# A gated expert layer and FFN: the FFN's first layer as seven products of quarters, over blocks of 1024 tokens

## The chip, the cores and the metric

The kernel runs on one core of a Trainium2 chip. A core has a matrix engine (TensorE, PE in the profile, with its weight loads shown apart as PEld), a vector engine (VectorE, DVE), an engine for activation functions and copies (ScalarE, ACT), a general engine (GpSimd, POOL) and a queue engine that issues DMAs (SyncE, SP). They run their own instruction streams in order and wait for one another by semaphores. Matrix products are written to PSUM[...]; everything else lies in SBUF. The metric is the device time of one execution in microseconds (us); before the change it is 289.29 us, the median of three runs (288.32 to 289.66).

## The reference

Input x is 4 x 512 tokens of 512 numbers. Two layers follow, each with a residual and a gate:

```python
x = x + tanh(g_xattn) * xattn(layernorm(x), ids, ctx, ctx, ctx)
x = x + tanh(g_ffn) * ffn(layernorm(x), w1, w3, w2, wr)
```

In xattn every token has one of four experts by its id (three bounds: 6250, 12500, 18750). Expert e is the 512 x 512 matrix ctx[e], used three times: g = silu(h ctx[e]^T), u = h ctx[e]^T, y = (g * u) ctx[e]^T. In ffn, h = silu(silu(h w1^T) w3^T) w2^T for all 2048 tokens, with 512 x 512 matrices, and a router (softmax of h wr^T, the best two of eight) gives two gates a token. `out.at[indices].add(gates * h)` adds those rows to rows 0 to 7 of the output, so that all tokens end in eight rows: the second layer's outputs can be summed by gate first and multiplied by w2 once.

## The kernel before

The tokens are sorted by expert into 17 passes of 128 rows. Thirteen passes (0 to 12) belong wholly to one expert each and need one matrix; four (13 to 16) hold the rests in groups of 32 rows and need four matrices, one for each group. The tables for this (`padded`, `lanes`, `atlane`, `what`, `tok`, lines 178 to 330) are computed on DVE at the start; `tok`, a product in PSUM, is the list of rows, from which `from_row` (gather) and `to_row` (scatter) are made. Meanwhile `busy(n)` gives PE filler products.

A pass p goes through: `gather` (POOL, an indirect DMA, line 393), `centre` (DVE: statistics and subtraction), `turn_in` (four PE transposes into a PSUM tile "tp", an ACT copy to hT), `up` (product z with the matrix, line 457; silu on ACT; a DVE multiply gives g), `turn_mid` (transposes of g, copy to gT), `down` (product y with the same matrix; DVE adds it to x, line 485; POOL scatters the row to the output), `norms` (DVE: the second layer norm), and `turn_out` (transposes, and ACT copies into hT2, the FFN's input; for a pass of 32-row groups four small copies to computed columns, line 533).

`load(p)` puts the matrices of a pass, 1 MB each, on SP's queue into the buffers of pool `mp` (8). A matrix is used by `up` and by `down`, and its buffer is free when `down` has read it; SP waits for that in its own order.

The order of the work is written out by hand and each engine runs in the order of the program. `order` is 0 to 6, 13, 7, 8, 14, 9, 10, 15, 11, 12, 16; "index" below is a place in this list, and the loop (lines 747 to 768) does for i: up(i), turn_in(i+1), centre(i+2), gather and load(i+3), down(i-1), turn_out(i-2), norms, a step of the FFN, turn_mid(i), another step. A step is the next piece of `ffn(b)`, a generator for a block of 512 tokens which enters the list `running` once all its passes are turned out (before: at i = 5, 10, 16 and 18). Its pieces are: four of the first layer (product u with w1, four matmul calls over 512 tokens, line 591, then silu into s1), one with the router's logits lg (line 604) and the routing on DVE, four of the second layer (product v with w3, line 618, silu into s2), and a short one in which the gated sums are added to `acc`. What has not run by the end of the loop runs after it. PSUM's eight banks are four for products ("mm": cnt, idle, tok, z, y, u, v, o in the order in which they are made), three for transposes and one for acc.

Of the kernel before, what the change touches and what calls it, by code (L numbers as in the profile page):

```python
# [8 lines left out]
F32 = mybir.dt.float32  # L9
BF16 = mybir.dt.bfloat16  # L10
F16 = mybir.dt.float16
I32 = mybir.dt.int32
AF = mybir.ActivationFunctionType
ALU = mybir.AluOpType
# [4 lines left out]
P = 128  # L19
# [5 lines left out]
def tile_gated_moe_ffn(  # L25
# [50 lines left out]
    assert E == 4 and G == 4  # L76
    TB = 512
    NB = NT // TB
    TT = TB // P

    const = ctx.enter_context(tc.tile_pool(name="const", bufs=1))
    mp = ctx.enter_context(tc.tile_pool(name="mp", bufs=8))
    hp = ctx.enter_context(tc.tile_pool(name="hp", bufs=2))
    xp = ctx.enter_context(tc.tile_pool(name="xp", bufs=5))
    work = ctx.enter_context(tc.tile_pool(name="work", bufs=3))
    s1p = ctx.enter_context(tc.tile_pool(name="s1p", bufs=2))
    small = ctx.enter_context(tc.tile_pool(name="small", bufs=4))
    ps_mm = ctx.enter_context(tc.tile_pool(name="ps_mm", bufs=4, space=bass.MemoryType.PSUM))
    ps_tp = ctx.enter_context(tc.tile_pool(name="ps_tp", bufs=3, space=bass.MemoryType.PSUM))
    ps_acc = ctx.enter_context(tc.tile_pool(name="ps_acc", bufs=1, space=bass.MemoryType.PSUM))  # L90

    def ct_(shape, dtype, name):
        return const.tile(list(shape), dtype, tag=name, name=name)

# [32 lines left out]
    for e in range(1, E):  # L127
# [12 lines left out]
    H = 12  # L140
    lane = ct_([P, P, H], BF16, "lane")
    nc.gpsimd.iota(
        lane, pattern=[[1, P], [0, H]], base=0, channel_multiplier=0,
        allow_small_or_imprecise_dtypes=True,
    )
    passes = ct_([P, NP, NJ], F16, "passes")
    nc.gpsimd.iota(
        passes, pattern=[[P, NP], [0, NJ]], base=0, channel_multiplier=0,
        allow_small_or_imprecise_dtypes=True,
    )  # L150

# [38 lines left out]

    idle = ps_mm.tile([P, TB], F32, tag="mm", name="idle")

    def busy(n):
        for _ in range(n):
            nc.tensor.matmul(
                idle, ones, lane.rearrange("p a b -> p (a b)")[:, 0:TB], start=True, stop=True
            )

# [29 lines left out]

    terms = ct_([P, 3, E, NJ], F32, "terms")
    over = ct_([P, E, NJ], F32, "over")  # L230
    nc.vector.tensor_tensor(over, rank_in, wide(size[:, 0, :]), ALU.is_ge)
    jump = ct_([P, E], F32, "jump")
    nc.vector.tensor_sub(jump, cut[:, E : 2 * E], cut[:, 1 : E + 1])
    nc.vector.tensor_mul(terms[:, 0], rank_in, hot)
    nc.vector.tensor_mul(over, over, hot)
    nc.vector.tensor_tensor(terms[:, 1], hot, wide(cut[:, 0:E]), ALU.mult)
    nc.vector.tensor_tensor(terms[:, 2], over, wide(jump), ALU.mult)
    padded = ct_([P, NJ], I32, "padded")
    with nc.allow_low_precision("whole numbers below 4096"):
        nc.vector.tensor_reduce(padded, terms.rearrange("p h e j -> p j (h e)"), AX.X, ALU.add)  # L240
    inpass_i = ct_([P, NJ], I32, "inpass_i")
    nc.vector.tensor_single_scalar(inpass_i, padded, -P, op=ALU.bitwise_and)

    start = ct_([P, 2 * E - 1], F32, "start")
    nc.vector.scalar_tensor_tensor(start, cut[:, 1 : 2 * E], 0.0, steps, ALU.is_le, ALU.mult)
    lanes = ct_([P, NJ], BF16, "lanes")
    nc.vector.tensor_sub(lanes, padded, inpass_i)
    which0 = ct_([P, 1], I32, "which0")
    with nc.allow_low_precision("whole numbers below 4096"):
        nc.vector.tensor_reduce(which0, start, AX.X, ALU.add)  # L250
    atlane = [ct_([P, P, n], F16, f"atlane{n}") for n in (H, NJ - H)]

# [9 lines left out]
    at_lane(0)  # L262
    inpass = ct_([P, NJ], F16, "inpass")
    nc.vector.tensor_copy(inpass, inpass_i)
    what = ct_([P, NP, NJ], F16, "what")
# [35 lines left out]

    busy(25)
    from_row = ct_([P, NP], I32, "from_row")
# [6 lines left out]
    def row_tables():  # L310
# [19 lines left out]
        )  # L330


    hT2 = {NB - 1: ct_([P, KC, TB + Q], F32, "hT2")}
    acc = ps_acc.tile([P, D], F32, tag="acc", name="acc")
# [76 lines left out]
    def turn_in(p):  # L411
        tp = transposed(hs.pop(p), f"a{p}")
        hTs[p] = work.tile([P, KC * P], F32, tag="hT", name=f"hT_{p}")
        nc.scalar.copy(hTs[p], tp)

    def first_in(p):

        st = small.tile([P, 6], F32, tag="st", name=f"st_a{p}")
        nc.vector.bn_stats(st, xs[p])
        mvs[p] = small.tile([P, 2], F32, tag="mv", name=f"mv_a{p}")  # L420
        nc.vector.bn_aggr(mvs[p], st)
        hTs[p] = work.tile([P, KC * P], F32, tag="hT", name=f"hT_{p}")
        n = D // 2
        for i in range(2):
            h = work.tile([P, n], F32, tag="h", bufs=4, name=f"h_a{p}_{i}")
            nc.vector.tensor_scalar(
                h, xs[p][:, i * n : (i + 1) * n], mvs[p][:, 0:1], None, ALU.subtract
            )
            tp = ps_tp.tile([P, n], F32, tag="tp", name=f"tp_a{p}_{i}")
            for k in range(n // P):  # L430
                nc.tensor.transpose(tp[:, k * P : (k + 1) * P], h[:, k * P : (k + 1) * P], ident)
            nc.scalar.copy(hTs[p][:, i * n : (i + 1) * n], tp)  # L432
# [32 lines left out]
    def up(p, inside=None):  # L465
        z = ps_mm.tile([P, D], F32, tag="mm", name=f"z_{p}")
        expert_product(z, hTs.pop(p), p, inside)
        g = work.tile([P, D], F32, tag="g", name=f"g_{p}")
        rs = rss.pop(p)
        nc.scalar.activation(g, z, AF.Silu, scale=rs)  # L470
        nc.vector.scalar_tensor_tensor(g, z, rs, g, ALU.mult, ALU.mult)  # L471
        gs[p] = g

    def turn_mid(p):
        tp = transposed(gs.pop(p), f"g{p}")
        gT = work.tile([P, KC * P], F32, tag="gT", name=f"gT_{p}")
        nc.scalar.copy(gT, tp)
        gTs[p] = gT
# [35 lines left out]
    def turn_out(p):  # L514

        tp = transposed(hs2.pop(p), f"f{p}").rearrange("p (k t) -> p k t", k=KC)
        if p < NF:
            b = p // TT
            if b not in hT2:
                hT2[b] = hp.tile([P, KC, TB], F32, tag="hT2", name=f"hT2_{b}")  # L520
            nc.scalar.copy(hT2[b][:, :, p % TT * P : (p % TT + 1) * P], tp)  # L521
            return
# [11 lines left out]

    def route(b, lg):


# [23 lines left out]

        lt = small.tile([P, TT, Q], F32, tag="lt", bufs=2, name=f"lt_{b}")
        nc.vector.transpose(lt.rearrange("p t q -> p (t q)"), lg)  # L563
        l1 = lt[:, :, 0:NR]
# [18 lines left out]

    def ffn(b):

        hT = hT2.pop(b)
        s1 = s1p.tile([P, KC, TB], F32, tag="s1", name=f"s1_{b}")
        for m in range(KC):
            u = ps_mm.tile([P, TB], F32, tag="mm", name=f"u_{b}_{m}")
            for k in range(KC):  # L590
                nc.tensor.matmul(  # L591
                    u,
                    w1[:, k, m * P : (m + 1) * P],
                    hT[:, k, 0:TB],
                    start=(k == 0),
                    stop=(k == KC - 1),
                )
            nc.scalar.activation(s1[:, m, :], u, AF.Silu)  # L598
            yield
        lg = ps_tp.tile([P, P], F32, tag="tp", name=f"lg_{b}")  # L600
        for k in range(KC):
            cols = hT[:, k, 0:TB].rearrange("p (t c) -> p t c", t=TT)
            for i in range(P // Q):
                nc.tensor.matmul(  # L604
                    lg[i * Q : (i + 1) * Q, :],
                    wr[:, k, :],
                    cols[:, :, i * Q : (i + 1) * Q],
                    start=(k == 0),
                    stop=(k == KC - 1),
                )  # L610
        g = route(b, lg)
        yield
        def gated(t, half=None):

            c0, n = (0, D) if half is None else (half * D // 2, D // 2)
            v = ps_mm.tile([P, n], F32, tag="mm", name=f"v_{b}_{t}_{c0}")
            for k in range(KC):
                nc.tensor.matmul(  # L618
                    v,
                    s1[:, k, t * P : (t + 1) * P],  # L620
                    w3[:, k, c0 : c0 + n],
                    start=(k == 0),
                    stop=(k == KC - 1),
                )
            s2 = work.tile([P, n], F32, tag="s2", bufs=5, name=f"s2_{b}_{t}_{c0}")
            nc.scalar.activation(s2, v, AF.Silu)  # L626
            return s2

        def add(t, s2):
# [4 lines left out]
                start=(b == 0),  # L634
                stop=(b == NB - 1 if t < TT - 2 else b == NB - 2),
            )
# [12 lines left out]
        s2s = []  # L649
        if b < NB - 1:  # L650
            for t in range(TT):
# [9 lines left out]
        for t in range(TT - 2):  # L661
            add(t, s2s[t])
        a = work.tile([P, D], F32, tag="a", bufs=1, name="a")
        nc.scalar.copy(a, acc)
# [39 lines left out]
    SHORT = 1  # L704
    last = {b: max(i for i, p in enumerate(order) if min(p // TT, NB - 1) == b) for b in range(NB)}
    running = []

# [39 lines left out]
    for i in range(2, NP + 2):  # L747
# [16 lines left out]
        step()  # L764
        running += [ffn(b) for b in range(NB) if last[b] == i - 2]
        if i < NP:
# [55 lines left out]
```

## Time and profile before

| | |
|---|---|
| median of three runs | 289.29 us |
| profiled execution | 289.3 us, its span (first to last instruction) 287.6 us |
| granted TensorE clock, mean | 0.997 |
| PE busy | 278.1 us (97%) |
| DVE busy | 128.9 us (45%) |
| ACT busy | 63.9 us (22%) |
| POOL busy | 38.8 us (14%) |
| first layer, u (L591), PE | 57.1 us |
| second layer, v (L618), PE | 57.3 us |
| expert products z and y (L457), PE | 61.8 and 61.4 us |
| DMA | 42.54 MB, mean 148 GB/s over the span |

A line of instructions in the profile names the source line, the engine, the operation, output and inputs, partitions x elements, and a count; then the busy time, the mean of one in ns, and the idle time just before, with what ended it. "A<-B" means that A is made from B. The mean of one matmul is longer than the step from one to the next, because matmuls overlap; steps are read from the times at which they start.

### The profile page before, as it was taken

The numbers are of one execution on the slowest core, as the hardware profiler recorded it, in microseconds if no ns is written. First come the engines' busy times: TensorE is split into PE (matmuls) and PEld (weight loads), VectorE is DVE, ScalarE is ACT, GpSimd is POOL, SyncE is SP. The second block draws the span as 40 slices with busy tenths as digits, with TensorE's granted clock in tenths as the row PEclk, the third lists the DMA queues.
The fourth block names the chain that finished last, engine by engine and source line by source line (L and its number), as shares of the span: only waits on it lengthen the run. The fifth ranks groups of instructions, "written<-read, shape, count | busy, mean of one in ns | idle before, by whom it ended". The sixth has DMA issues, their size and how long they took to land.

```text
span 287.6 us, 3554 instructions
## 1 busy us (share of the span) xinstructions
PE 278.1 (97%) x1192; PEld 129.1 (45%) x1193; DVE 128.9 (45%) x573; ACT 63.9 (22%) x122; POOL 38.8 (14%) x62
## 2 busy tenths in 40 slices
PE   4999999999999999999999999999999999999994
PEld 1444455554434544434444445444443454344463
DVE  4379878773707660807270866170533431001300
ACT  2015221332111322213212232212321221111120
POOL 6420122221111111111111111010110100000000
PEclk9999999999999999999999999999999999999998
DMA  0575999996512349622359634044000000000000
GB/s 1 190 285 186 384 391 390 391 391 252 201 55 113 106 177 397 232 78 93 126 160 385 232 98 182 0 157 171 36 0 36 13 0 1 0 0 2 0 1 2
DMA packets 20722, 42.54 MB, mean 148 GB/s; under 512 B 2143, under 2 KB 2207, under 8 KB 20704
## 3 DMA queue, kind: packets, MB, share of 16 engines
q1 hardware_dynamic: 17664, 33.66, 32.4%
q0 software_dynamic: 2720, 8.65, 8.3%
q8 instruction: 9, 0.15, 0.2%
q14 instruction: 9, 0.07, 0.1%
q10 hardware_dynamic: 320, 0.01, 0.1%
HBM read 38.10 MB, written 4.47 MB: 148 GB/s over the span
## 4 chain that ended last, share of the span: by engine, by line
PE 90%; DVE 4%; DMA 3%; issue 1%; ACT 0%; POOL 0%; DVEq 0%
PE y L457 21%; PE u L591 19%; PE v L618 19%; PE z L457 18%; PE tp_f L384 3%; PE tp_a L384 2%; PE tp_g L384 2%; DMA x<-in_x_dram,from_row 2%; PE acc L630 2%; PE lg L604 1%; DMA idt<-in_ids_dram 1%; PE accT L640 1%; PE o L694 0%; ACT hT L521 0%; PE tok L275 0%
## 5 line engine op out<-in xcount | busy, mean ns | idle before, releaser
L457 PE MATMUL z<-m,hT 128*32 128x512 f32 (+1 forms) x232 | 61.8, 595 | 0.2 <-ACT hT L432 0.2
L457 PE MATMUL y<-m,gT 128*32 128x512 f32 (+1 forms) x232 | 61.4, 594 | 0.0
L591 PE MATMUL u<-hT,w 128*128 128x512 f32 x128 | 57.1, 595 | 0.5 <-ACT hT L521 0.5
L618 PE MATMUL v<-w,s 128*128 128x512 f32 (+1 forms) x136 | 57.3, 570 | 0.0
L471 DVE SCALAR_TENSOR_TENSOR g<-z,rs_a,g 128x512 f32<-128x512 f32 x17 | 12.8, 750 | 62.6 <-ACT g L470 62.6
L457 PEld LDWEIGHTS z<-m,hT 128*32 128x32 f32 (+1 forms) x232 | 22.9, 146 | 30.8 <-issue 29.6
L618 PEld LDWEIGHTS v<-w,s 128*128 128x128 f32 x136 | 24.9, 190 | 25.5 <-issue 24.9
L591 PEld LDWEIGHTS u<-hT,w 128*128 128x128 f32 x128 | 23.4, 190 | 27.1 <-issue 26.2
L457 PEld LDWEIGHTS y<-m,gT 128*32 128x32 f32 (+1 forms) x232 | 22.5, 146 | 27.9 <-issue 27.9
L486 POOL DMA_INDIRECT out_dram<-x,to_row x17 | 16.9, 993 | 111.3 <-DVE x L485 110.1
L393 POOL DMA_INDIRECT x<-in_x_dram,from_row x17 | 16.6, 976 | 73.6 <-issue 25.2
L485 DVE SCALAR_TENSOR_TENSOR x<-y,tg,x 128x512 f32<-128x512 f32 x17 | 12.8, 751 | 22.2 <-PE y L457 22.2
L470 ACT ACTIVATE g<-z,rs_a 128x512 f32<-128x512 f32 x17 | 11.7, 687 | 38.3 <-PE z L457 38.3
L598 ACT ACTIVATE s<-u 128x512 f32<-128x512 f32 x16 | 9.6, 597 | 47.2 <-PE u L591 47.2
L626 ACT ACTIVATE s<-v 128x512 f32<-128x512 f32 (+1 forms) x17 | 9.7, 572 | 41.3 <-PE v L618 41.3
L563 DVE STREAM_TRANSPOSE lt<-lg 128x128 f32<-128x128 f32 x4 | 1.3, 317 | 37.1 <-PE lg L604 37.1
L521 ACT COPY hT<-tp_f 128x512 f32<-128x512 f32 x13 | 7.6, 586 | 42.7 <-PE tp_f L384 42.7
L384 PEld LDWEIGHTS tp_f<-ident,h_f 128*128 128x128 f32 x68 | 8.2, 141 | 10.2 <-issue 10.2
L344 DVE BATCH_NORM_STATS2 st_a<-x 128x6 f32<-128x512 f32 x16 | 11.0, 686 | 3.4 <-DMA x<-in_x_dram,from_row 3.4
L344 DVE BATCH_NORM_STATS2 st_f<-x 128x6 f32<-128x512 f32 x17 | 11.8, 694 | 0.6
L384 PEld LDWEIGHTS tp_a<-ident,h_a 128*128 128x128 f32 x64 | 7.7, 141 | 9.5 <-issue 7.8
L384 PEld LDWEIGHTS tp_g<-ident,g 128*128 128x128 f32 x68 | 8.1, 140 | 7.4 <-issue 6.1
(140 smaller groups left out, 205.5 us busy)
## 6 DMA issues: line engine op xcount, KB each, us to landing
m<-in_ctxT_dram SPq DMA_DIRECT2D x29, 1024.0 KB
w<-in_w1T_dram SPq DMA_DIRECT2D x1, 1024.0 KB
w<-in_w3T_dram SPq DMA_DIRECT2D x1, 1024.0 KB
w<-in_w2T_dram SPq DMA_DIRECT2D x1, 1024.0 KB
x<-in_x_dram,from_row POOLq DMA_INDIRECT x17, 5.9
out_dram<-x,to_row POOLq DMA_INDIRECT x17, 6.0
wr<-in_wrT_dram SPq DMA_DIRECT2D x1, 64.0 KB
x_first<-out_dram SPq DMA_DIRECT2D x4, 4.0 KB
```

Source lines behind the costliest of these rows:

```text
L344: nc.vector.bn_stats(st, xt)
L384: nc.tensor.transpose(tp[:, k * P : (k + 1) * P], h[:, k * P : (k + 1) * P], ident)
L393: nc.gpsimd.indirect_dma_start(out=xt, out_offset=None, in_=x, in_offset=bass.IndirectOffsetOnAxis(ap=from_row[:, p : p + 1], axis=0),)
L457: nc.tensor.matmul(out_ps[i * n : (i + 1) * n, :], lhs[:, k * P + i * n : k * P + (i + 1) * n], m[:, k, :], start=(k == 0), stop=(k == KC ...
L470: nc.scalar.activation(g, z, AF.Silu, scale=rs)
L471: nc.vector.scalar_tensor_tensor(g, z, rs, g, ALU.mult, ALU.mult)
L485: nc.vector.scalar_tensor_tensor(xt, y, tg[:, 0:1], xt, ALU.mult, ALU.add)
L486: nc.gpsimd.indirect_dma_start(out=out, out_offset=bass.IndirectOffsetOnAxis(ap=to_row[:, p : p + 1], axis=0), in_=xt, in_offset=None, bou ...
L591: nc.tensor.matmul(u, w1[:, k, m * P : (m + 1) * P], hT[:, k, 0:TB], start=(k == 0), stop=(k == KC - 1),)
L598: nc.scalar.activation(s1[:, m, :], u, AF.Silu)
L618: nc.tensor.matmul(v, s1[:, k, t * P : (t + 1) * P], w3[:, k, c0 : c0 + n], start=(k == 0), stop=(k == KC - 1),)
L626: nc.scalar.activation(s2, v, AF.Silu)
```

## The change

The FFN's first layer is done over two blocks of 1024 tokens. w1 and the block's input are cut in quarters (halves of the outputs or tokens, halves of the 512 inputs), and the four quarters of the result come from seven products of quarters in place of eight. The sums of quarters are made beforehand: four of w1 on POOL, S1 to S4 (`sums_of_w1`, in iteration i = 4), and four of the input on DVE, T1 to T4 (`sums_of_hT`, for each block when it enters `running`). A part of the later sums is made by accumulating several products in one PSUM tile: X takes four of them and is copied out by ACT after the first (c1) and the second (u2), Y takes two with a copy after the first (c7), and Z one. Where a copy must be added, DVE adds it to the PSUM tile before ACT's silu. One step does two products, so that the first layer has seven steps of four matmul calls for a block.

The logits of both halves come first, in one step, into the two X tiles. The second layer runs over halves of 512 tokens as it did.

PSUM's banks are two for "mm", two for X and the logits, one for Y, two for transposes and one for acc. In SBUF the matrices have six buffers in place of eight, hT, gT and g have two in place of three, s2 four in place of five; the position tables lie in a pool that is closed after use, and the tiles of the first layer (`ffp`) take its place.

In the tables, lane, pass and position are 16-bit integers where they were bf16, f16 and 32-bit integers; the place is summed over experts before it is masked by `hot`, so that the reduction has 64 elements in place of 192, and a cast is gone. The filler is fed by `ones` in place of `lane`, and its second run has 21 in place of 25 products.

```diff
-    TB = 512
+    TB = 1024
     NB = NT // TB
-    TT = TB // P
+    HB = TB // 2
+    TT = HB // P
...
-    mp = ctx.enter_context(tc.tile_pool(name="mp", bufs=8))
+    mp = ctx.enter_context(tc.tile_pool(name="mp", bufs=6))
...
-    ps_mm = ctx.enter_context(tc.tile_pool(name="ps_mm", bufs=4, space=bass.MemoryType.PSUM))
-    ps_tp = ctx.enter_context(tc.tile_pool(name="ps_tp", bufs=3, space=bass.MemoryType.PSUM))
+    ps_mm = ctx.enter_context(tc.tile_pool(name="ps_mm", bufs=2, space=bass.MemoryType.PSUM))
+    ps_x = ctx.enter_context(tc.tile_pool(name="ps_x", bufs=2, space=bass.MemoryType.PSUM))
+    ps_y = ctx.enter_context(tc.tile_pool(name="ps_y", bufs=1, space=bass.MemoryType.PSUM))
+    ps_tp = ctx.enter_context(tc.tile_pool(name="ps_tp", bufs=2, space=bass.MemoryType.PSUM))
...
-    lane = ct_([P, P, H], BF16, "lane")
...
-    passes = ct_([P, NP, NJ], F16, "passes")
...
+    lane = ct_([P, P, H], I16, "lane")
...
+    passes = ct_([P, NP, NJ], I16, "passes")
...
-    nc.vector.tensor_mul(terms[:, 0], rank_in, hot)
-    nc.vector.tensor_mul(over, over, hot)
-    nc.vector.tensor_tensor(terms[:, 1], hot, wide(cut[:, 0:E]), ALU.mult)
-    nc.vector.tensor_tensor(terms[:, 2], over, wide(jump), ALU.mult)
...
-        nc.vector.tensor_reduce(padded, terms.rearrange("p h e j -> p j (h e)"), AX.X, ALU.add)
...
+    place = ct_([P, E, NJ], F32, "place")
+    nc.vector.tensor_tensor(place, rank_in, wide(cut[:, 0:E]), ALU.add)
+    nc.vector.tensor_tensor(over, over, wide(jump), ALU.mult)
...
+    nc.vector.tensor_add(place, place, over)
...
+    nc.vector.tensor_mul(place, place, hot)
+    padded = ct_([P, NJ], I16, "padded")
+    with nc.allow_low_precision("whole numbers below 4096"):
+        nc.vector.tensor_reduce(padded, place.rearrange("p e j -> p j e"), AX.X, ALU.add)
+    lanes = ct_([P, NJ], I16, "lanes")
+    nc.vector.tensor_single_scalar(lanes, padded, P - 1, op=ALU.bitwise_and)
+    inpass = ct_([P, NJ], I16, "inpass")
+    nc.vector.tensor_single_scalar(inpass, padded, -P, op=ALU.bitwise_and)
...
-    inpass = ct_([P, NJ], F16, "inpass")
-    nc.vector.tensor_copy(inpass, inpass_i)
...
-    busy(25)
+    busy(21)
...
+    positions.close()
+    ffp = ctx.enter_context(tc.tile_pool(name="ffp", bufs=1))
...
+        nc.gpsimd.tensor_add(ss[0], a21, a22)
+        nc.gpsimd.tensor_sub(ss[1], ss[0], a11)
+        nc.gpsimd.tensor_sub(ss[2], a11, a21)
+        nc.gpsimd.tensor_sub(ss[3], a12, ss[1])
...
+        nc.vector.tensor_sub(ts[0], b12, b11)
+        nc.vector.tensor_sub(ts[1], b22, ts[0])
+        nc.vector.tensor_sub(ts[2], b22, b12)
+        nc.vector.tensor_sub(ts[3], b21, ts[1])
...
+        def product(out_ps, a, bb, c, start):
+            for k in range(2):
                 nc.tensor.matmul(
-                    u,
-                    w1[:, k, m * P : (m + 1) * P],
-                    hT[:, k, 0:TB],
...
+                    out_ps,
+                    a[:, k, c * P : (c + 1) * P],
+                    bb[:, k, :],
...
+        def active(m, half, ps, other=None):
+            to = s1[:, m, half * HB : (half + 1) * HB]
+            if other is not None:
+                nc.vector.tensor_add(to, ps, other)
+                ps = to
+            nc.scalar.activation(to, ps, AF.Silu)
+
+        def p1(c):
+            xs_[c] = ps_x.tile([P, HB], F32, tag="x", name=f"X_{b}_{c}")
+            product(xs_[c], a11, b11, c, True)
+            c1s[c] = kept(xs_[c], "c1", c)
+
+        def p2(c):
+            z = ps_mm.tile([P, HB], F32, tag="mm", name=f"Z_{b}_{c}")
+            product(z, a12, b21, c, True)
+            active(c, 0, z, c1s.pop(c))
+
+        def p6(c):
+            product(xs_[c], sa2, t2, c, False)
+            u2s[c] = kept(xs_[c], "u2", c)
+
+        def p7(c):
+            ys[c] = ps_y.tile([P, HB], F32, tag="y", name=f"Y_{b}_{c}")
+            product(ys[c], sa3, t3, c, True)
+            c7s[c] = kept(ys[c], "c7", c)
+
+        def p5(c):
+            product(xs_[c], sa1, t1, c, False)
+            active(2 + c, 1, xs_[c], c7s.pop(c))
+
+        def p4(c):
+            product(ys[c], a22, t4, c, False)
+            active(2 + c, 0, ys.pop(c), u2s.pop(c))
+
+        def p3(c):
+            product(xs_[c], sa4, b22, c, False)
+            active(c, 1, xs_.pop(c))
+
+        todo = [
+            (p1, 0), (p2, 0), (p1, 1), (p2, 1), (p6, 0), (p7, 0), (p5, 0),
+            (p4, 0), (p3, 0), (p6, 1), (p7, 1), (p5, 1), (p4, 1), (p3, 1),
+        ]
...
+        lg = ps_x.tile([P, P], F32, tag="x", name=f"lg_{b}_{half}")
...
+        lts = [logits(b, half) for half in range(2)]
         yield
+        yield from first_layer(b)
+        for half in range(2):
+            yield from second_layer(2 * b + half, route(2 * b + half, lts[half]))
...
-        running += [ffn(b) for b in range(NB) if last[b] == i - 2]
+        for b in range(NB):
+            if last[b] == i - 2:
+                hT_sums[b] = sums_of_hT(b)
+                running.append(ffn(b))
+        if i == 4:
+            w1_sums = sums_of_w1()
```

## The prediction

> **What bounds the kernel now.** I read the page's busy shares first, then its chain, then the costliest groups.
>
> ```profile
> PE 278.1 (97%) x1192; PEld 129.1 (45%) x1193; DVE 128.9 (45%) x573; ACT 63.9 (22%) x122; POOL 38.8 (14%) x62
> ...
> PE 90%; DVE 4%; DMA 3%; issue 1%; ACT 0%; POOL 0%; DVEq 0%
> ...
> L591 PE MATMUL u<-hT,w 128*128 128x512 f32 x128 | 57.1, 595 | 0.5 <-ACT hT L521 0.5
> ```
>
> TensorE (PE) is busy for 97% and carries 90% of the chain that ends last; from 25 us on the chain is PE alone but for two 0.6 us waits for an ACT copy. So a removed matmul counts in full, and so does every new idle on PE. The row also says that one f32 matmul call is two instructions: 4 blocks x 4 x 4 = 64 calls, 128 rows. The chain in order of time (start, length, what) gives the pace of a pass of the experts that has no FFN work beside it:
>
> ```profile
> 46.83 3.43 PE z L457 x8
> 50.27 0.44 PE tp_a L384 x4
> 50.70 3.44 PE y L457 x8
> 54.14 0.44 PE tp_f L384 x4
> 54.58 0.44 PE tp_g L384 x4
> ```
>
> 3.44 us for 8 instructions is 0.43 us each; four transposes take 0.44; a pass takes 8.2 us. Two more views matter, because matrix buffers fall from 8 to 6: what the SP queue waits for (total, times, longest), and the DMA by microsecond (clock, share, GB/s) after the down product of order index 7, the first pass with four matrices.
>
> ```profile
> SPq L447 <- PE y L457: 122.2, 11, 14.4
> ```
>
> ```profile
> 99.17 3.57 PE y L457 x32
> ```
>
> ```profile
> 103.00:104.00 1.00, 1.00 0.10 35
> 104.00:105.00 1.00, 1.00 0.51 190
> 105.00:106.00 1.00, 1.00 1.02 397
> ...
> 115.00:116.00 1.00, 1.00 1.05 393
> 116.00:117.00 1.00, 1.00 0.72 264
> 117.00:118.00 1.00, 1.00 0.00 0
> ```
>
> Matrix loads wait for a down product to free their buffer. With 8 buffers (numbered in load order, one per matrix), matrices 15 to 18 wait for index 7's four, freed at 102.73. The burst that answers starts 1.8 us later and ends at 116.7: 14.0 us for four matrices of 1 MB plus a gather and a scatter of rows. PE doesn't notice: the next product with four matrices starts at 125.68.
>
> [...] the filler's weight loads come 0.43 us apart until 12.6 us, and from 12.96 on 17 of them take 3.55 us[...] The compare L255 (bf16 in, f16 out) does 1536 elements in 957 ns[...]; int16 no run here shows.
>
> **The change, part by part.**
>
> *Seven products for eight.* A block of 1024 tokens takes 7 x 2 x 2 = 28 calls where it took 32; over both, 8 calls = 16 instructions of 0.43 us are gone: **-6.9 us**, all on the path. The logits stay 64 calls, the second layer is untouched.
>
> *The sums around them.* VectorE (DVE): twelve additions of PSUM to SBUF at about 0.75 us (row of L485: 751 ns for 128x512). ACT: twelve copies at 0.59 (L521's row), 7 us. Both engines have room (45% and 22% busy), and X, Y and Z alternate so that two to four matmul calls (0.86 us each) lie between a product and the one that needs its copy read: cost 0; without that cover each would cost 0.7 to 0.9. POOL: four sums of w1 of 512 elements. No row shows one[...]. They stand in POOL's queue behind the scatter that ends at 56.5 and before the gather that starts at 62.33, in an idle of 5.8 us: 0. If they took 2 us each, the gather and its DVE row statistics would be 2 us late, and PE perhaps 1.
>
> *T1 to T4 on DVE*, four subtractions of 1024 f32 elements per block. From L285 (216 elements, 376 ns) and a 64-element row (L231, 225 ns): 225 + 960 x 0.99 = 1.18 us, 1.22 with the step between, 4.9 for four. For block 0 they lie behind index 9's norms; g of index 11 and the logits' transposes are queued behind them, and PE has z of index 11, a transpose and y of index 10 (7.3 us) to do: 0. For block 1 nothing is left beside them:
>
> ```profile
> 232.86 0.60 PE L384 MATMUL tp_f<-ident,h_f 128*128 128x128 f32 x4
> ```
>
> ```profile
> 234.84 0.27 ACT L533 COPY hT<-tp_f 128x128 f32 x1 [0.16 <-ACT hT L533]
> ```
>
> The last ACT copy ends at 235.11, 1.65 us after the last transpose. Before, block 2's second layer (four 3.44 us steps) followed and hid this. After, I count the steps: block 0 needs 1 + 7 + 4 + 4, and the loop offers 16 before the last turn_out; only four accumulations (1.0) are left. Counted from the transpose's end: accumulations to 1.0, logits two times 1.0, so PE has 3.0 us of work. T1 starts at 1.75, T4 ends at 6.65, and only then come the logits' transposes in DVE's queue (0.32, L563). The first product needs the X buffer that the first logits hold: the pool has two, both with logits. It starts at 7.0. **+4.0 us** idle, wherever the logits stand in it. Ends: 3.3[...] to 4.6.
>
> *FFN starts later.* Block 0 now needs index 8, not 3, so the loop's i = 5 to 9 have no FFN step. PE is full at 8.2 us a pass then, as above, and DVE's 7.6 us fit. But cover goes. With six buffers, the four matrices of index 10 (numbers 13 to 16) wait for index 7's (7 to 10) all at once. From index 7's down product to index 10's up product PE has: two transposes, z, transpose, y, two transposes: 5 x 0.44 + 2 x 3.44 = 9.1 us. The loads need what the same four took above, 14.0; with one more gather or scatter in it (0.26 MB at 393 GB/s, 0.7) 14.7. I take 14.3: **+5.2 us**, ends 4.0 and 6.2. The product's first sub-product wants all four matrices, so none of it runs ahead. Earlier loads fit: index 7's last matrix waits for index 4, freed at 62.3, lands by 68 and is wanted at 71.4. Indices 13 and 16 have FFN steps in their window again (23 us): 0.
>
> *Four product buffers in PSUM become two.* In the head, cnt, idle, tok, z of pass 0, z of pass 1 now go 0, 1, 0, 1, 0: z of pass 1 must wait until DVE has read tok for the last time.
>
> ```profile
> 20.80 3.68 PE L457 MATMUL z<-m,hT 128*128 128x512 f32 x8
> ```
>
> ```profile
> 22.61 0.18 DVE L314 SCALAR_TENSOR_TENSOR to_row<-tok,pad 128x17 int32<-128x17 f32 x1
> ```
>
> ```profile
> 24.49 0.14 issue
> 24.63 0.63 PE tp_g L384 x4
> ```
>
> Six of these eight instructions are z of pass 1, from 21.65; now they start at 22.83 and end at 25.41, where tp_g stood at 24.63 (DVE's g at 24.49 held it): **+0.8 us**. In the loop the product before the last is always evacuated in time: 0. Three transpose buffers to two, and hT, gT, g with two: the same answer.
>
> *Positions.* Before at_lane: one reduction of 64 instead of 192 elements (259 for 475 ns), otherwise as many operations: -0.16; the cast before `what` goes: -0.19. [...]**-0.35 us** on the path to the gathers[...]. busy(21) for 25 ends four fillers of 0.21 earlier, which DVE's chain (x of pass 1, then tok's readers) swallows: 0.
>
> *Fresh waits.* An operand awaited at the start of a product costs 0.26 (3.70 for 3.44 us at 63.43) and up to 0.2 before it: one such place goes (index 12's block), three come (z of pass 1, z of index 10, first product of block 1): **+0.3**.
>
> Sum: -6.9 + 4.0 + 5.2 + 0.8 - 0.35 + 0.3 = **+3.1 us**: a span of 290.7 after 287.6. The profiled execution took 289.3 with 1.7 outside its span, and the median of the runs is 289.29, so **292.4 us**.
>
> **Rivals.**
> (1) *The matrices come in time.* If DMA answers within 9.1 us of the release, the 5.2 go and the result is 287.2, faster by 0.7%. For it: DMA is otherwise idle there. Against it: four matrices at 393 GB/s are 10.7 us without latency. It turns to faster when they take less than 9.7 us. 0.08.
> (2) *Tail hidden.* If the logits' transposes don't stand behind the T's, or X isn't what the product waits for, 4.0 shrink to the 0.7 us of the copies: 289.1, no change. Against: DVE runs in the program's order everywhere in this trace. 0.10. Both (1) and (2): 283.9, 0.02.
> (3) *The clock drops* in one of the two long idle stretches: [...] with the sum above 294 to 296. [...] Against: in the first, single sub-products run as the matrices land[...]. 0.22.
>
> **Numbers.** The forecast keeps 0.58, with its own range from the ends above: 290 to 295.5. About 0.5% (1.45 us) is what a measurement here can tell. Faster: (1), both, and a little of (2): 0.11. Same: the rest of (2) and the low end of the forecast: 0.15. Slower: 0.74. The range from 288.2 to 297 leaves out the faster cases and two drops together with high ends.
>
> **What would show it.** PE loses 16 instructions of 128x512 in the first layer; in the loop z of index 10 (x32) starts after about 5 us of idle, with SP's wait on y just before; the chain shows DVE T's near the end and PE waiting for the transpose of lg; z of pass 1 waits for tok's reader. If PE is idle in neither place, the result is near 284 and I am wrong; if small gaps appear in every pass from 55 to 97 us, DVE had become the bound, which I exclude by 7.6 of 8.2 us.

## The result and the profile after

The changed kernel takes 297.53 us (median of four runs, 295.94 to 299.02) where the kernel before takes 289.38 in the same comparison: a ratio of 1.0288, 95% interval 1.0225 to 1.035. The forecast was slower, 292.4 us, and its range ended at 297.0. The sign was right and the time lies outside the range: 8.2 us were lost where 3.1 were forecast. The profiled execution of the changed kernel took 296.94 us with a span of 295.2, against a span of 287.6 before.

The same parts of the page, after: busy shares, the granted clock in 40 slices, the chain by engine, and two groups.

```profile
PE 275.8 (93%) x1173; PEld 127.4 (43%) x1173; DVE 148.6 (50%) x592; ACT 70.9 (24%) x134; POOL 44.3 (15%) x66
...
PEclk9999999999999979999999999999999799999998
...
PE 77%; DMA 11%; DVE 8%; issue 2%; ACT 1%; SPq 0%; ACTq 0%; POOLq 0%; DVEq 0%
...
L459 PE MATMUL z<-m,hT 128*32 128x512 f32 (+1 forms) x232 | 66.8, 628 | 6.3 <-DMA m<-in_ctxT_dram 4.7
...
L620 PE MATMUL X<-hT,w 128*128 128x512 f32 x16 | 9.2, 706 | 3.6 <-DVE lt L697 3.6
```

PE still does most of the chain, but 11% of it is now DMA and 8% DVE. Busy time fell by only 2.3 us, although 16 instructions of 0.43 us are gone: z has become 5 us longer with as many instructions (61.8 to 66.8), nearly all of it at index 10, as shown below. The two 7s in the clock row are slices of 7.4 us in which PE ran partly at half its clock. The two groups carry the idle: z waits for matrices, and X for a transpose of the logits.

The chain in order of time, at index 10 (start, length, what):

```profile
84.23 3.57 PE y L459 x32
...
88.38 0.45 PE tp_g L386 x4
...
91.10 13.63 DMA m<-in_ctxT_dram
104.73 0.04 issue
104.77 5.32 PE z L459 x26
```

Index 7's down product frees four buffers at 87.80. The last of index 10's matrices lands at 104.73, 16.9 us later, where PE had 9.1 us of work. The product z of such a pass is 32 instructions, eight for each matrix and its group of 32 rows. PE's timeline (idle before, and what ended it, in brackets) shows that six of them ran early, as the first three matrices came in:

```profile
96.93 2.10 PE L459 MATMUL z<-m,hT 128*32 128x512 f32 x4
100.69 1.04 PE L459 MATMUL z<-m,hT 128*32 128x512 f32 x2 [1.67 <-DMA m<-in_ctxT_dram]
```

Nothing was gained by that: all 32 together take 3.64 us in the kernel before, and the last 26 alone take 3.62 at full clock in the runs below. Here these 26 take 5.32, 1.7 us more. With the 3.1 us that now stand on record for the first six, this is nearly all of the 5 us by which z has grown. The matching stretch by microsecond (PE busy, clock, DMA share, GB/s):

```profile
102.00:103.00 1.00, 0.00 (x0) 1.00 1.02 381
103.00:104.00 1.00, 0.00 (x0) 1.00 1.04 397
104.00:105.00 1.00, 0.23 (x4) 1.00 1.05 410
105.00:106.00 1.00, 1.00 (x8) 0.59 1.02 385
106.00:107.00 1.00, 1.00 (x11) 0.50 0.17 64
107.00:108.00 1.00, 1.00 (x12) 0.50 0.25 43
108.00:109.00 1.00, 1.00 (x12) 0.70 0.65 221
```

From 95 us to the end of the wait the DMA moves 381 to 418 GB/s: it was late because more was asked of it than fits in the time. PE has work again at 104.77; from 105.2 to 108.6 its granted clock is 0.50. The chain at the tail:

```profile
226.18 1.24 DVE T L598
227.44 1.22 DVE T L599
228.67 1.14 DVE T L600
229.80 1.13 DVE T L601
230.94 0.24 DVE lt L697
...
231.22 3.57 PE X L620 x4
234.79 1.83 PE Z L620 x4
236.62 1.72 PE X L620 x4
```

This is the forecast wait, T1 to T4 and then the transpose that frees X; again the product after it takes about twice its time (3.57 us, where the third takes 1.72), with a granted clock of 0.50 from 231.5 to 234.9. The DMA moves nothing from 230 to 237 us, so that its load isn't what lowers the clock here.

### The profile page after: what moved, and what is told of

Same layout as the page of the kernel before. It is cut to its first block, busy times and chain, and to the rows that moved or that the text cites. A ratio compares the mean times of both kernels' runs of the same rounds, so it can differ in the third digit from the quotient of the medians.

```text
span 295.2 us, 3567 instructions
## 1 busy us (share of the span) xinstructions
PE 275.8 (93%) x1173; PEld 127.4 (43%) x1173; DVE 148.6 (50%) x592; ACT 70.9 (24%) x134; POOL 44.3 (15%) x66
## 4 chain that ended last, share of the span: by engine, by line
PE 77%; DMA 11%; DVE 8%; issue 2%; ACT 1%; SPq 0%; ACTq 0%; POOLq 0%; DVEq 0%
PE v L719 19%; PE z L459 16%; PE y L459 15%; PE X L620 10%; PE Y L620 5%; DMA m<-in_ctxT_dram 5%; DMA x<-in_x_dram,from_row 3%; PE Z L620 2%; DMA out_dram<-x,to_row 2%; PE tp_f L386 2%; PE tp_g L386 2%; PE tp_a L386 2%; PE acc L731 1%; DMA idt<-in_ids_dram 1%; DVE q_a L375 1%
## 5 line engine op out<-in xcount | busy, mean ns | idle before, releaser
L459 PE MATMUL z<-m,hT 128*32 128x512 f32 (+1 forms) x232 | 66.8, 628 | 6.3 <-DMA m<-in_ctxT_dram 4.7
L620 PE MATMUL X<-T,S 128*128 128x512 f32 x32 | 15.0, 592 | 0.0
L639 ACT ACTIVATE s<-s 128x512 f32<-128x512 f32 x12 | 7.6, 630 | 22.4 <-DVE s L637 22.4
L620 PE MATMUL X<-hT,w 128*128 128x512 f32 x16 | 9.2, 706 | 3.6 <-DVE lt L697 3.6
L479 ACT COPY gT<-tp_g 128x512 f32<-128x512 f32 x17 | 9.9, 585 | 6.2 <-PE tp_g L386 6.1
L637 DVE TENSOR_TENSOR s<-X,c 128x512 f32<-128x512 f32 x4 | 2.8, 692 | 16.2 <-PE X L620 16.2
```

The source lines that it names most:

```text
L459: nc.tensor.matmul(out_ps[i * n : (i + 1) * n, :], lhs[:, k * P + i * n : k * P + (i + 1) * n], m[:, k, :], start=(k == 0), stop=(k == KC ...
L620: nc.tensor.matmul(out_ps, a[:, k, c * P : (c + 1) * P], bb[:, k, :], start=start and k == 0, stop=k == 1, skip_group_check=True,)
```

## The experiments

The theory after the trace: two waits on PE and the half clock that follows each make the loss, and the seven products keep their worth. The rivals: the DMA is too slow whatever is asked for when; the six buffers alone are the loss; the half clock has a cause of its own; the seven products are worth less than their instructions. All kernels below are compared with runs of the kernel before on the same chip (289.3 to 289.4 us).

**The four-matrix pass one place earlier**, in the changed kernel:

```diff
-    order = [0, 1, 2, 3, 4, 5, 6, NF, 7, 8, ...
+    order = [0, 1, 2, 3, 4, 5, NF, 6, 7, 8, ...
```

> The changed kernel with one edit: pass 13 (four matrices) stands one place earlier in the order, at index 6 in place of 7, so that its four buffers are freed a pass (8.2 us) earlier while index 10 still wants them at the same time. Theory: the 7.7 us idle before z of index 10 is the release of four buffers at once with too little work behind it, and the half clock after it (z 5.32 us for 3.57) follows from the idle. Then both go: idle under 1 us, full clock, -9.4 us, about 288. Rival: the loads are late because the DMA engines share their rate with the row transfers and other loads, whenever they start; then several us of the idle stay, about 293 to 297.

Measured: 292.27 us, ratio 1.011 (1.0088 to 1.0131): 5.3 us gained of the 9.4 expected. Two lines of PE in order of time say what is left:

```profile
97.34 1.06 PE L459 MATMUL z<-m,hT 128*32 128x512 f32 x6
100.73 3.62 PE L459 MATMUL z<-m,hT 128*32 128x512 f32 x26 [2.33 <-DMA m<-in_ctxT_dram]
```

The last matrix still comes 3.4 us after PE could have used it (97.34 to 100.73), in place of 7.8; the idle right before it is 2.33 us, and after it z runs at full clock in this execution (granted 1.00 in each microsecond from 96 to 116). I had overlooked that index 9's matrix now waits for the same release, so that five matrices are asked for within a pass; that this is why the wait isn't gone is argued here and tried out with pass 13 at index 5 below.

**The T's after the logits' transposes**, in the changed kernel. `sums_of_hT(b)` moves from the loop into `ffn(b)`, behind the two logits:

```diff
         lts = [logits(b, half) for half in range(2)]
+        hT_sums[b] = sums_of_hT(b)
         yield
...
-                hT_sums[b] = sums_of_hT(b)
                 running.append(ffn(b))
```

> The changed kernel with one edit: T1 to T4 of a block are issued on DVE after the transposes of the block's logits, not before them. Theory: the 3.6 us idle before the second block's first product is the X tile held by logits whose transposes stand behind 4.9 us of T's; it goes (under 0.5 us left), and so does the half clock after it (two products of 1.7 us took 5.4 in place of 3.4): -5.6 us, about 292. Rival: the idle only moves to the first product that reads a T (T2 ready 2 to 3 us later than before): 1 to 3 us of it stay, about 294 to 296.

Measured: 292.17 us, ratio 1.0092 (1.0075 to 1.0109), 5.4 us less than the changed kernel. The first product of the second block follows its logits with no idle, at full clock:

```profile
225.90 2.29 PE L689 MATMUL lg<-hT,wr 128*32 128x128 f32 x64
228.12 1.98 PE L620 MATMUL X<-hT,w 128*128 128x512 f32 x4
```

So 3.6 us of wait and 1.7 us of half clock hung on the order of five DVE instructions. The rival is out: no product waits for a T.

**Both edits together.**

> Both edits together: the four-matrix pass one place earlier and the T's behind the logits' transposes. Theory: the two waits are independent and both on the path, so the gains add: -15 us, about 282.5, which is faster than the kernel before by some 2.4%, close to the 6.9 us that sixteen matmul instructions are worth. Rival: PE becomes limited elsewhere (DVE in the stretch without FFN steps, ACT, PSUM buffers), and the sum of the gains is under 10 us: 287 or more.

Measured: 287.16 us, ratio 0.9924 (0.9898 to 0.9949): the two edits add up (5.3 + 5.4 = 10.7, measured 10.4), and the kernel is now 0.8% faster than the one before. It is 4.7 us short of the forecast 282.5; that is at index 10 and not in another engine, where its profile has the last matrix 3.6 us late, 2.50 us of it idle right before it, and 5.28 us for the rest of z. SP's issues show the load on the DMA: four matrices at once, and the last a pass later.

```profile
80.08 3.66 SPq L449 DMA_DIRECT2D m<-in_ctxT_dram  x4
```

```profile
88.43 0.37 SPq L449 DMA_DIRECT2D m<-in_ctxT_dram  x1
```

The eleven runs lie between 284.79 and 288.87, a spread that the kernel before doesn't have. The granted clock goes with it: the four longest (287.88 and more) have a mean of 0.992 to 0.994, the seven others 0.997 to 1.0. So the half clock comes in some executions of this kernel and not in others.

**Filler in the two waits**, in the changed kernel: 14 products of `ones` before up(order[10]) and again after the second block's logits.

```diff
+        if i == 10:
+            filler(14, "idle_a")
         if i < NP:
             up(order[i])
...
         lts = [logits(b, half) for half in range(2)]
+        if b == NB - 1:
+            filler(14, "idle_b")
         yield
```

> The changed kernel with 14 filler products (0.21 us each at full clock, results unused, in the Y bank) put on PE before z of index 10 and again after the second block's logits: the two waits stay as they are, but PE is busy for some 3 us of each. Theory: the half clock comes from the idle time; z of index 10 still starts its last sub-products when the fourth matrix lands, but at full clock, likewise the first products of block 2: -3.7 us, about 293.8. Rival: the half clock has another cause (the load of the DMA, or the clock unit's own timing); z of index 10 and the first X product take 5.3 and 3.6 us as now, and the time stays at 297 to 298.

Measured: four runs from 291.43 to 297.73, median 296.69; as a time, this decides nothing. The trace, of an execution of 297.25 us, says more. In order of time, PE:

```profile
97.24 3.19 PE L703 MATMUL idle_a<-ones 128*128 128x512 bf16 x14
100.36 1.90 PE L459 MATMUL z<-m,hT 128*32 128x512 f32 x6
105.24 6.55 PE L459 MATMUL z<-m,hT 128*32 128x512 f32 x26 [2.98 <-DMA m<-in_ctxT_dram]
```

```profile
229.58 3.19 PE L703 MATMUL idle_b<-ones 128*128 128x512 bf16 x14
233.26 1.98 PE L620 MATMUL X<-hT,w 128*128 128x512 f32 x4 [0.48 <-DVE lt L697]
```

At the tail the filler left 0.48 us of idle, and X runs at full clock (1.98 us, granted 1.00), though it starts as late after the T's as without filler: what differs is that PE was busy, so the half clock there hangs on the idle. At index 10 the filler stood too early: it ran in the first 3 us of the wait, and the 2.98 us before the last matrix stayed idle and were followed by half clock for even longer (granted 0.50 from 104.4 to 111.2). I had miscounted what the filler would fill.

**Six buffers alone**, in the kernel before:

```diff
-    mp = ctx.enter_context(tc.tile_pool(name="mp", bufs=8))
+    mp = ctx.enter_context(tc.tile_pool(name="mp", bufs=6))
```

> The kernel before with six matrix buffers in place of eight, nothing else. Theory: six buffers alone cost nothing there, because the FFN steps of the first block stand between index 7's down product and index 10's up product (23 us of PE work for a need of 14 to 17): within 0.5 us of the kernel before. Rival: the buffers alone are the loss, wherever the FFN stands: 3 us or more slower, with PE waiting for m.

Measured: 289.37 us, ratio 1.0001 (0.9992 to 1.001), and no wait for m. The buffers alone cost nothing. That they cost something in the changed kernel because its FFN steps no longer stand between index 7 and index 10 is argued from the order of the work; no run here moves those steps alone.

**Seven buffers**, in the changed kernel: `mp` with 7, and `h` with 3 in place of 4.

> The changed kernel with seven matrix buffers in place of six (and three buffers for h in place of four, to make room). Theory: one of index 10's four matrices then takes the buffer of index 6, freed a pass earlier, so that three, not four, are asked for at 87.8 us: about 3 us less idle, -3 us, about 294.5, with the half clock still in most executions. Rival: the DMA's rate is the bound from 80 us on, whatever is asked for when; then nothing is gained, 297.5.

Measured: 291.86 us, ratio 1.009 (1.0065 to 1.0115), 5.7 us less than with six. The last matrix comes 3.2 us after PE could have used it (97.24 to 100.48) in place of 7.8, which is 4.6 us where I had expected 3. The rest is the clock, which I had left at half: after 1.70 us of idle z runs at full clock (granted 1.00).

```profile
100.48 3.62 PE L459 MATMUL z<-m,hT 128*32 128x512 f32 x26 [1.70 <-DMA m<-in_ctxT_dram]
```

**The four-matrix pass at index 5**, with the T's moved:

```diff
-    order = [0, 1, 2, 3, 4, 5, 6, NF, 7, 8, ...
+    order = [0, 1, 2, 3, 4, NF, 5, 6, 7, 8, ...
```

> The T's behind the logits' transposes, as before, and pass 13 at index 5 in place of 6: of index 10's four matrices two are then freed by index 5's down product, one each by index 6's and 7's, and only the last (1 MB) has a single pass behind it. Theory: in the kernel with both edits the 2.5 us idle that was left at index 10 is five matrices (index 9's too) and five row transfers asked for within one pass and a half, at the 0.39 MB per us that the DMA gives; spread over three passes they land before 97 us, the idle goes, and with it the half clock and the spread between runs: 282.5 to 283.5. Rival: the idle comes from something else in the DMA (a fixed share for row transfers, the order in the queue) and stays at 2 us or more: 286 to 287.

Measured: 282.95 us, ratio 0.9787 (0.9761 to 0.9814). Index 10 doesn't wait any more. In its place index 5 has a short wait, at full clock after it:

```profile
58.29 3.62 PE L459 MATMUL z<-m,hT 128*32 128x512 f32 x26 [1.41 <-DMA m<-in_ctxT_dram]
```

**The sums of w1 one in each pass**, on top of that (S1 in i = 4, S2 in i = 5, and so on).

```diff
-        if i == 4:
-            w1_sums = sums_of_w1()
+        if 4 <= i < 8:
+            next(summing)
```

> As the one with pass 13 at index 5, and the four sums of w1 on POOL issued one in each of the iterations i = 4 to 7, not all four in i = 4. Theory: the 0.85 us that PE waits for h_f near 62 us is DVE held up by POOL's additions (four of its operations there take 1 to 2 us for 0.2); one addition a pass (1.3 us) fits in what DVE has free: -0.8 us. Rival: DVE is full in these passes anyway, and PE waits as much in sum, in several places: no change.

Measured: 284.43 us, ratio 0.9829 (0.9809 to 0.9849): no gain, and 1.5 us more than the kernel it was built on, whose five runs fall in two groups (282.7 to 283.0 and 284.3 to 284.9). It tests less than I meant: index 5's wait for its matrix already stands where PE would have waited for h_f. I can't say what parts the two groups; their granted clocks are 0.999 to 1.0 and 0.997.

**tok's last readers ahead of the large table**, on top of that: `pad` and `to_row` before `matrix_table(2, NU)`.

```diff
+    pad = ct_([P, NP], F32, "pad")
+    nc.vector.tensor_scalar(pad, tok, 1.0, float(4 * NT), ALU.is_lt, ALU.mult)
+    nc.vector.scalar_tensor_tensor(to_row, tok, -1.0, pad, ALU.add, ALU.add)
     matrix_table(2, NU)
```

> As the one with the sums spread, and the two DVE operations that read tok last (the scatter's rows) moved ahead of the large matrix table, so that PSUM's product buffer comes free 1.2 us earlier. Theory: the 1.5 us that PE waits before z of pass 1 is that buffer; z of pass 1 starts when hT is copied, near 20.4 in place of 21.7 us, and -1.0 us comes out at the end (g of pass 0 is next, at 23.3). Rival: DVE's g of pass 0 moves back by as much as the tables move forward, and nothing is gained.

Measured: 284.09 us, ratio 0.9823 (0.9803 to 0.9843), not told from the one before. The mechanism is right and the gain isn't there: z of pass 1 starts at 20.24 in place of 22.55, its wait shrinks from 1.89 to 0.17 us, but z of index 5 waits for the same DMA afterwards: PE is ready for it at 53.51 in place of 55.45, and its last part starts at 57.15 in place of 57.84.

**w3 and w2 loaded later**, on top of that: from before the loop to i = 4, behind the matrix of index 7.

```diff
-    w3 = load_w(w3T, "w3")
-    w2 = load_w(w2T, "w2")
     for i in range(2, NP + 2):
...
             load(order[i + 3])
+        if i == 4:
+            w3 = load_w(w3T, "w3")
+            w2 = load_w(w2T, "w2")
```

> As the one with tok's readers moved ahead, and the loads of w3 and w2 (1 MB each, first used after 140 us) moved on SP's queue from before the loop to i = 4, behind the matrix of index 7. Theory: the 1.4 to 1.6 us that PE waits at index 5 for its fourth matrix is a full DMA queue (390 GB/s from 30 to 56 us), 2 MB of which isn't needed yet; without them the matrix lands 5 us earlier and the wait goes: -1.5 us, about 282.5. Rival: the matrix waits for its buffer, not for the DMA, and nothing changes: 284.

Measured: 280.93 us, ratio 0.9716 (0.9687 to 0.9744): 3.2 us less than the kernel it was built on, more than the 1.5 expected. The 1.5 was only the idle right before the last matrix, which came 3.6 us after PE could have used it (53.51 to 57.15 above): the head's gain had gone into that wait, and now it comes out. The view of PE's waits (total, times, longest) has no matrix in it and nothing above 1 us after the start:

```profile
PE cnt L190 <- DVE hot L187: 4.1, 1, 4.1
PE tok L273 <- DVE what L267: 0.9, 1, 0.9
PE tp_a L429 <- DVE h_a L424: 0.8, 1, 0.8
PE z L455 <- DVE to_row L834: 0.5, 1, 0.5
...
```

This version beats both kernels, by 2.8% and 5.6%.

**Eight products in the mended kernel.** The first layer as plain products again (u, four k for each of eight steps), without T, S, X, Y and Z; all else as in the one just shown.

```diff
-        a11, a12, a22, (sa1, sa2, sa3, sa4) = w1_sums
...
+        for half in range(2):
+            for m in range(KC):
+                u = ps_mm.tile([P, HB], F32, tag="mm", name=f"u_{b}_{half}_{m}")
+                for k in range(KC):
+                    nc.tensor.matmul(
+                        u,
+                        w1[:, k, m * P : (m + 1) * P],
+                        hT2[b][:, k, half * HB : (half + 1) * HB],
+                        ...
+                nc.scalar.activation(s1[:, m, half * HB : (half + 1) * HB], u, AF.Silu)
+                yield
```

> The kernel with late w3 and w2 and all waits mended, with the first layer as plain products: eight steps of four matmul calls for a block of 1024 tokens, no T and S sums, no X, Y, Z, silu from PSUM. Theory: with no wait left on PE, the seven products are worth exactly their sixteen instructions: this is 6.9 us slower than the one with seven products, about 289.5. Rival: the sums, copies and additions cost something on the path even now (DVE, ACT, PSUM buffers), so that the difference is under 5 us; or part of the gain over the kernel before came from the other edits, and this one is faster than the kernel before.

Measured: 288.09 us, ratio to the kernel before 0.9962 (0.9951 to 0.9973), and 7.2 us more than with seven products. The sums, copies and additions cost nothing that shows on the path; the seven products are worth what their 16 instructions are. The second half of the rival came true in part: with eight products this kernel is 1.2 us faster than the one before, so of the 8.4 us that separate the version above from the kernel before, 7.2 are the seven products and 1.2 the other edits; the next run has 1.0 for the position tables alone.

**The position tables alone**, in the kernel before (with the filler's edits).

```diff
-    lane = ct_([P, P, H], BF16, "lane")
...
+    lane = ct_([P, P, H], I16, "lane")
...
-    busy(25)
+    busy(21)
```

> The kernel before with the change's position tables alone: 16-bit integers, the shorter reduction, the filler fed by ones with 21 products. Theory: tok comes 0.35 us earlier, and the first matrix 0.8 to 1.0 us earlier because its number is ready sooner, so that the second gather's rows land ahead of it; in the changed kernel g of pass 0 came 1.2 us earlier than before: -1.2 us, 288.2. Rival: only the 0.35 us count: 289.0, not told from no change.

Measured: 288.35 us, ratio 0.997 (0.9958 to 0.9982), 1.0 us gained for 1.2 expected. The second gather's rows are there earlier by three times the 0.35 us that tok gained (the statistics of pass 1 start at 16.61, where they started at 17.93).

## Why the prediction was wrong

Two steps failed: the half clock, which the sum put at nothing (3.4 us), and the landing of index 10's four matrices, which it put too early (2.6 us). A stall of DVE beside POOL, also put at nothing, adds 0.8. Part by part:

*Seven products: right.* -6.9 forecast, -7.2 measured with no other wait in the way.

*The sums: the engines right, one queue wrong.* DVE's additions, ACT's copies and the accumulations in X and Y stay off the path, and T takes 1.22 us, as worked out. POOL's four sums took 1.26 to 1.46 us each and fitted their time; what I left out is that some of DVE's instructions stand still beside them. In the changed kernel:

```profile
57.38 2.08 DVE L375 SCALAR_TENSOR_TENSOR q_a<-r_a,v_a 128x1 f32<-128x1 f32 x1
```

```profile
58.12 1.30 POOL L587 TENSOR_TENSOR S<-w 128x512 f32<-128x512 f32 x1
```

An operation of 0.2 us takes 2.08, and ends with POOL's first sum. In the kernel with the sums spread over four passes the stalls have moved with them, one in each of the four (1.96, 1.27, 1.27 and 1.81 us), each ending with its sum, so it is the sums that cause them. The third pair is:

```profile
75.99 1.30 POOL L592 TENSOR_TENSOR S<-w 128x512 f32<-128x512 f32 x1
```

```profile
76.05 1.27 DVE L367 SCALAR_TENSOR_TENSOR q_f<-r_f,v_f 128x1 f32<-128x1 f32 x1
```

In the changed kernel h_f comes late, and PE loses 0.8 us near 62 us (z of index 6 starts at 63.7; two passes of 8.2 after 46.5 is 62.9). Costed at 0. DVE itself was not the bound: in a pass without FFN work it was busy for 6.2 of 8.2 us before the change, less than the 7.6 that I had counted.

*T1 to T4 at the tail: right.* 4.0 us forecast, 3.6 measured, by the mechanism named, shown by moving them.

*FFN starts later: the mechanism right, the size wrong.* This is one of the two steps that failed. I took the landing from a burst before, 14.0 us for four matrices, one gather and one scatter, and took 14.3 for a part of one more row transfer. It was 16.9 us. By the view by microsecond, 5.74 MB moved between release and landing, where the burst before moved 4.74. POOL's issues show two gathers and two scatters in the time (88.27, 89.55, 97.65, 98.93), 0.26 MB each, so that 0.5 MB are left for index 11's matrix, which SP issued at 96.16. The extra 1.0 MB are 2.5 us at 0.4 MB per us, an estimate; the remaining 0.4 us are from 92 to 95 us, where the DMA moved only 244 to 338 GB/s, and why is open. Lateness is 16.9 - 9.1 = 7.8 us for 5.2 forecast; the top of my own range was 6.2. That none of z runs ahead was wrong, six instructions did, but it cost nothing.

*The clock: the rival that came true, twice.* This is the other step that failed, and the larger. After its first product PE never waits longer than 0.6 us in the kernel before, so that its trace couldn't price an idle of several us: the 0.22 for half clock after one of the two waits, and the time with it, were an estimate of mine. It came after both. At index 10, after 3.03 us of idle, it cost 1.7 us (5.32 for 3.62); at the tail, after 3.60 us, it cost 1.7 again (3.57 + 1.83 us for the first two products, which take 1.98 + 1.72 in the run with filler). Together that is 3.4. With 2.6 from the landing and 0.8 from DVE's stall, 6.8 us more were lost than forecast.

*The head: the mechanism right, the sign of the sum wrong.* z of pass 1 waited for tok's reader as said (1.4 us of idle), but the tables gained more than 0.35 (no run had shown 16-bit integers then, so that this was an estimate), and y of pass 0 starts at 26.29 where it started at 26.59: -0.3 for +0.45. With the two bubbles of about 0.45 us of the first layer's blocks before, both gone, and 0.4 at the tail, that is some 2 us less than forecast.

Against the spans: -6.9 (products) - 0.3 (head) + 0.8 (h_f) + 7.8 + 1.7 (index 10) + 3.6 + 1.7 (tail) + 0.3 (fresh waits, as forecast) - 0.9 (bubbles) = +7.8; measured +7.6.

What is open: what decides whether half clock comes after an idle of some 2.5 us, and the two groups of runs of the kernel with index 5.

## What to carry to other kernels

On a kernel whose chain is one engine, a removed instruction is worth its time only if the buffers that pay for it (matrices, PSUM, transposes) still leave enough work between a release and the next use: count that work in us, and count every transfer that shares the DMA in the same stretch, other queues and the next load included. An instruction that frees a buffer should be issued ahead of long ones that nothing waits for yet; here five DVE instructions in another order were worth 5.4 us. And read the granted clock behind every wait of PE: in the executions profiled here, products at about half speed followed idles of 2.50 to 3.61 us and cost 1.4 to 2.9 us on top of the wait; after idles of 1.33 to 2.33 us they ran at full speed.

## What the runs showed of the hardware

By the granted clock, a stretch of half clock lasted 3.4 us in the changed kernel (105.2 to 108.6 and 231.5 to 234.9), with the T's moved (105.0 to 108.4) and with both edits (100.9 to 104.3), and 6.8 in the run with filler (104.4 to 111.2); where a microsecond is partly at half clock, the end is worked out from its mean. In products with four matrices, the idle right before the last matrix, the time since z's first instruction, and the time of the remaining 26 instructions of z were:

| kernel | idle, us | since z's first, us | z's rest, us |
|---|---|---|---|
| tok's readers ahead (index 5) | 1.61 | 3.64 | 3.62 |
| seven buffers | 1.70 | 3.24 | 3.62 |
| four-matrix pass at index 6 | 2.33 | 3.39 | 3.62 |
| both edits | 2.50 | 3.57 | 5.28 |
| T's moved | 2.88 | 7.71 | 5.24 |
| filler | 2.98 | 4.88 | 6.55 |
| changed kernel | 3.03 | 7.84 | 5.32 |

The idle divides these seven executions between 2.33 and 2.50 us; the time since z's first instruction doesn't, since 3.64 us was followed by full clock and 3.57 by half. At the tail, 3.60 to 3.61 us of idle were followed by a slow X each time (3.42 to 3.60 us in three kernels), 0.48 us by one of 1.98. That is one execution each, and the mean clocks of the runs with both edits (0.992 to 1.0) differ from run to run.

A compare of 16-bit integers with an f16 result took the time of one of bf16 (512 elements in 0.42 us, 1536 in 0.96, in both kernels). In the two bursts at index 7, row transfers and matrix loads together moved at 0.38 to 0.42 MB per us in most microseconds, and the burst with more bytes took longer (4.74 MB in 14.0 us before, 5.74 in 16.9 after).
